# A two-layer transformer with two mixtures of experts on one core: first scores and routing moved, expert tiles in four steps of five, gathers paced, projections dense

## The chip, the cores and the metric

The kernel runs on one core of a Trainium2 chip. The metric is the device time of one execution in microseconds (us), as a median over runs. PE is TensorE, DVE is VectorE, ACT is ScalarE, POOL is GpSimd, SP is the engine that issues most transfers. All data is float32.

## The reference

The input is `x` of 8 sequences, 256 tokens each, 128 features: 2048 tokens. Layer 0 and layer 1 have the same frame: normalise, then add attention and a feed-forward network of the normalised tokens to `x`.

```python
xn = layernorm(x)
x = x + attn0(xn) + ffn0(xn)
xn = layernorm(x)
x = x + attn1(xn) + ffn1(xn)

# attn0: 16 heads of 8; q, k, v with biases; softmax(q k^T / sqrt(8)) v, then Wo and bo
# ffn0:  top 2 of 8 experts (width 176, silu(g)*u), weights are the softmax scores,
#        plus sigmoid(x w) * shared expert (width 352)
# attn1: 8 query heads of 128, one k/v head, sinusoidal positions, causal
# ffn1:  top 1 of 8 experts (width 512, gelu), times its softmax score;
#        router logits are (x wg_red^T) (wg / |wg|)^T
```

## The kernel before, in words

Tokens are 16 tiles of 128, or 4 blocks of 512. `acc` holds the residual, 16 tiles in SBUF; `xT` holds the normalised tokens transposed.

**Start.** `layernorm` takes statistics on DVE, the inverse root as a power on POOL, `xn` on DVE (L252), transposes on PE and copies into `xT` on ACT; it also writes `xn` to a DRAM table `xd` for later gathers. `l0_values` makes values `va` and router logits `lg0`. After the four blocks come the gate weights of layer 1 (`l1_gate_weights`), the router (`l0_router`: softmax, the two largest of 8), and the queries and keys of the first block (`l0_project(0)`).

**Routing.** The tokens of each expert are packed into slots of 128, at most 40 of them (`NS0`), each slot being one expert's. `routing` is a generator: counts by matmul (L312), positions by scans, then for each of two choices four rounds of one-hot tiles on DVE (L388, L395, L401) and matmuls (L406) which give `ids`, the token of each slot row. It is run between the first scores of sequence 0, two at a time, and finished before anything else begins. Then the first four slots' tokens are gathered (`slot_tokens`, indirect DMAs from POOL, L423), and weights of the first nine slots are loaded.

**Attention 0 in 64 steps.** Per sequence there are 4 head groups of 4 heads and two halves: 8 steps. A head has a strip of 32 partitions. The scores are made twice: `max_scores` (L726), one sequence ahead, whose row maxima (`max_rows`, L741) are written as a column of `mx`; `l0_augment` transposes `mx` and adds it to the queries (`qa`, L752), so that the second scores (`exp_scores`, L769) come out with the maximum taken off and transposed for the values; `exponentials` is on ACT (L781), `l0_pv` (L796) multiplies by `va`. First scores of sequence b+1 and second scores of sequence b use different strips of the array and are issued in turns. Two score buffers of two PSUM banks (`big`) serve both, three single banks (`bank`) serve all else.

**What goes between steps.** `between(step)` runs after each step's scores. Steps 3 to 43: one expert tile per step (`l0_down` of the last tile, L589; `l0_up`, L572; `l0_turn` of the next, L565). Step 43: the results of tokens 0 to 7 tiles are gathered back (`l0_back`, two gathers each), and each further one when `l0_combine` (L613) has used a buffer; there are 8 (`YT`). Steps 44 to 59: the shared expert (`shared_up` L628, `shared_down` L643). Steps 50 to 57: two `l0_combine` each. Steps 53, 55, 59: `layernorm` of layer 1. From 56: `l1_project` of its first block.

**Layer 1** follows: attention with one k/v head, the expert tiles of layer 1 in its middle, gathers, output. No line of it is in the diff but what it shares with layer 0.

Order within an engine is fixed when the program is built: a scheduler interleaves the calls within limits set by buffers and data. The order of both kernels' instructions can be listed engine by engine, and the prediction uses this.

Of the kernel before, what the change touches and what calls it, by code (L numbers as in the profile page):

```python
# [47 lines left out]

TILES = 3
SHARED = TILES + NS0 + 1  # L50
COMBINE = SHARED + 6
NORM1 = (COMBINE + 3, COMBINE + 5, COMBINE + 9)
PROJECT1 = COMBINE + 6
EPS_LN = 1e-5
# [5 lines left out]
def two_layer_kernel(  # L60
# [56 lines left out]
    minus_half = ctile([P, TPB], "minus_half")  # L117
    nc.gpsimd.memset(minus_half, -0.5)
    rev = ctile([P, NE], "rev")
    for e in range(NE):  # L120
# [43 lines left out]

    bv0_s = ctile([P, E], "bv0_s")
    bo0_s = ctile([P, E], "bo0_s")
    qb0_s = ctile([P, NG], "qb0_s")
    kb0_s = ctile([P, NG], "kb0_s")
    nc.gpsimd.dma_start(bv0_s, bv0.partition_broadcast(P))
    nc.gpsimd.dma_start(qb0_s, qb0)  # L170
# [49 lines left out]

    wqkp = wp.tile([P, 2, H0, ROW], F32, tag="wqk", name="wqkp")
    wqp, wkp = wqkp[:, 0], wqkp[:, 1]
    for padded, plain in ((wqp, wq0_s), (wkp, wk0_s)):
        nc.vector.memset(padded, 0.0)
        nc.vector.tensor_copy(padded[:, :, :D0], plain.rearrange("p (h d) -> p h d", d=D0))

# [11 lines left out]
    def layernorm(layer, blk):  # L238
# [8 lines left out]
        nc.gpsimd.tensor_scalar_add(rs, mv[:, :, 1], EPS_LN)  # L247
        nc.gpsimd.tensor_tensor(rs, rs, minus_half, ALU.pow)
        xn = work.tile([P, TPB, E], F32, tag="xn", name=f"xn_{nm}")
        ps = bank(f"lnT_{nm}")  # L250
        for t in range(TPB):
            nc.vector.tensor_scalar(  # L252
                xn[:, t, :],
                acc[:, blk * TPB + t, :],
                mv[:, t, 0:1],
                rs[:, t : t + 1],
                ALU.subtract,
                ALU.mult,
            )
            nc.tensor.transpose(ps[:, ts(t, P)], xn[:, t, :], ident)  # L260
# [188 lines left out]
    def l0_values(blk):  # L449
        for t2 in range(blk * TPB, (blk + 1) * TPB, 2):  # L450
            ps = bank(f"vg_{t2}")
            pv = ps[:, : 2 * (E + NE + 1)].rearrange("p (t c) -> p t c", t=2)
            for t in range(2):
                nc.tensor.matmul(
                    pv[:, t, :], lhsT=xT[:, ts(t2 + t, P)], rhs=wvg0_s, start=True, stop=True
                )
            for t in range(2):
                nc.vector.tensor_tensor(
                    va[:, t2 + t, :, :D0],
                    pv[:, t, :E].rearrange("p (h d) -> p h d", d=D0),  # L460
                    bv0_s.rearrange("p (h d) -> p h d", d=D0),
                    ALU.add,
                )
            nc.scalar.copy(lg0[:, ds(t2, 2), :], pv[:, :, E:])

    def l0_project(blk):
        both = work.tile([P, 2, NG, BLK], F32, tag="qk", name=f"qk0_{blk}")
        qT, kT = both[:, 0], both[:, 1]
        for g in range(NG):
            for dst, w, bias in ((qT, wqp, qb0_s), (kT, wkp, kb0_s)):  # L470
                ps = bank(f"qk0_{blk}_{g}")
                nc.tensor.matmul(  # L472
                    ps,
                    lhsT=w[:, ts(g, 4), :],
                    rhs=xT[:, ts(blk, BLK)],
                    start=True,
                    stop=True,
                )
                if w is wqp:
                    nc.vector.tensor_scalar_add(dst[:, g, :], ps, bias[:, g : g + 1])  # L480
                else:
                    nc.scalar.activation(
                        dst[:, g, :], ps, AF.Identity, bias=bias[:, g : g + 1]
                    )
        qk[blk] = (qT, kT)

    for blk in range(NBLK):
        layernorm(0, blk)
        l0_values(blk)
        nc.gpsimd.tensor_tensor(  # L490
            acc[:, ts(blk, TPB), :],
            acc[:, ts(blk, TPB), :],
            bo0_s.unsqueeze(1).to_broadcast([P, TPB, E]),
            ALU.add,
        )


    def l1_gate_weights():
# [4 lines left out]
        n1 = small.tile([NE, 1], F32, tag="wg_n1", name="wg_n1")  # L503
        nc.scalar.activation(n1, n2, AF.Sqrt)
        nc.vector.tensor_scalar_max(n1, n1, EPS_WG)
# [12 lines left out]
        nc.vector.tensor_copy(wvg1_s[:, P:], ps2[:, :NE])  # L518

    l1_gate_weights()  # L520

# [18 lines left out]
    r0 = Routing()  # L540
    routing0 = routing("l0", l0_router(), NS0, r0)

# [67 lines left out]
    def l0_combine(t):  # L610
        a = acc[:, t, :]
        for k in range(2):
            nc.vector.scalar_tensor_tensor(  # L613
                a, yt0[t][:, k, :], wr0[:, t, k : k + 1], a, ALU.mult, ALU.add
            )
        if t + YT < NTILE:
            l0_back(t + YT)

# [67 lines left out]

    def between(step):

        i = step - TILES
        if 0 <= i - 1 < NS0:  # L690
            l0_down(i - 1)
        if 0 <= i < NS0:
            l0_up(i)
        if 0 <= i + 1 < NS0:
            l0_turn(i + 1)
        if i == NS0:
            for t in range(YT):
                l0_back(t)
        blk, c = divmod(step - SHARED, len(CH) + 1)
        if 0 <= blk < NBLK:  # L700
            if c < len(CH):
                shared_up(blk, c)
            else:
                shared_down(blk)
        if 0 <= step - COMBINE < NTILE // 2:
            for t in range(2):
                l0_combine(2 * (step - COMBINE) + t)
        if step in NORM1:
            layernorm(1, NORM1.index(step))
        if step >= PROJECT1:  # L710
            for _ in range(2):
                next(project1, None)

# [22 lines left out]
    def max_rows(b, i, ps):  # L736
# [4 lines left out]
        nc.vector.tensor_reduce(  # L741
            m[:, ds(2 * half, 2), :, D0 + g], pv, AX.X, ALU.max, negate=True
        )

    def l0_augment(b):
# [3 lines left out]
        for t in range(2):  # L749
            nc.tensor.transpose(ps[:, ts(t, P)], mx[b % 2][:, t, :], ident)  # L750
        qa = work.tile([P, NG, S], F32, tag="h", name=f"qa_{b}")
        nc.vector.tensor_tensor(  # L752
            qa,
            qT[:, :, ds((b % 2) * S, S)],
            ps[:, :S].unsqueeze(1).to_broadcast([P, NG, S]),
            ALU.add,
        )
        return qa
# [71 lines left out]

    NI = 2 * NG
    l0_project(0)
    for i in range(0, NI, 2):
        pair = [big_tile(f"s1_0_{i + h}") for h in range(2)]
        issue(*(max_scores(0, i + h, pair[h]) for h in range(2)))
        for h in range(2):
            max_rows(0, i + h, pair[h])
        for _ in range(5):
            next(routing0, None)
    for _ in routing0:  # L840
        pass
    xs0[0] = slot_tokens(0, 0, r0)
    for i in range(RING0):
        l0_weights(i)
    l0_turn(0)

# [7 lines left out]
    for b in range(B):  # L854
# [4 lines left out]
        for g in range(NG):  # L859
# [3 lines left out]
            for half in range(2):  # L863
# [10 lines left out]
                eTs.append(exponentials(b, i, ps2))  # L874
                between((b * NG + g) * 2 + half)
                if half == 0 and late is not None:
                    l0_drain(*late)
                    if g == 1 and done is not None:
                        l0_finish(*done)
                        done = None  # L880
            late = (b, g, eTs, po, at)
        done = (b, at)
    l0_drain(*late)
    l0_finish(*done)


# [332 lines left out]
```

## Time and profile before

| | us |
|---|---|
| median of 3 runs | 662.15 (660.63 to 668.9) |
| the profiled execution | 647.99 |
| its span, first to last instruction | 646.1 |
| PE busy in the span | 543.4 (84%) |
| DVE busy | 400.6 (62%) |
| ACT busy | 245.1 (38%) |
| POOL busy | 140.9 (22%) |
| mean granted PE clock | 0.934 |

The profiled execution is some 14 us shorter than the median. A busy PE is not PE at its peak: where the granted clock is low, the same work is busy for longer. Shares over the span are averages over very different stages, so stages are read one by one.

### The profile page before, as it was taken

The numbers are of one execution on the slowest core, as the hardware profiler recorded it, in microseconds if no ns is written. First come the engines' busy times: TensorE is split into PE (matmuls) and PEld (weight loads), VectorE is DVE, ScalarE is ACT, GpSimd is POOL, SyncE is SP. The second block draws the span as 40 slices with busy tenths as digits, with TensorE's granted clock in tenths as the row PEclk, the third lists the DMA queues.
The fourth block names the chain that finished last, engine by engine and source line by source line (L and its number), as shares of the span: only waits on it lengthen the run. The fifth ranks groups of instructions, "written<-read, shape, count | busy, mean of one in ns | idle before, by whom it ended". The sixth has DMA issues, their size and how long they took to land.

```text
span 646.1 us, 10887 instructions
## 1 busy us (share of the span) xinstructions
PE 543.4 (84%) x3797; PEld 380.6 (59%) x3797; DVE 400.6 (62%) x959; ACT 245.1 (38%) x649; POOL 140.9 (22%) x176
## 2 busy tenths in 40 slices
PE   1779599999999999945799777989898888489786
PEld 1537547766766676513355465667577887265564
DVE  6596437766676667745875598766674423357753
ACT  1210035444544454320322433234459945133442
POOL 9200252222222200775000000004023302700000
PEclk9995589999999999988899979898899999889999
DMA  8204113432444320111000005100029993300000
GB/s 206 71 1 122 40 39 97 111 107 64 118 110 112 51 28 29 45 50 54 18 8 9 6 12 135 50 2 25 8 54 260 247 231 84 86 8 2 8 9 8
DMA packets 53414, 44.01 MB, mean 68 GB/s; under 512 B 5153, under 2 KB 48225, under 8 KB 53361
## 3 DMA queue, kind: packets, MB, share of 16 engines
q1 hardware_dynamic: 48704, 35.09, 19.8%
q0 software_dynamic: 4080, 7.97, 6.2%
q8 instruction: 30, 0.49, 0.3%
q10 hardware_dynamic: 576, 0.27, 0.2%
q14 instruction: 24, 0.19, 0.1%
HBM read 35.97 MB, written 7.34 MB: 67 GB/s over the span
## 4 chain that ended last, share of the span: by engine, by line
PE 53%; DVE 14%; issue 14%; DMA 8%; POOL 6%; ACT 5%; POOLq 0%; SPq 0%; DVEq 0%; ACTq 0%
PE s L726 6%; PE s L1022 5%; PE u L572 5%; PE o L1065 5%; PE qk L668 4%; PE qk L472 4%; PE d L589 3%; PE pv L796 3%; POOL yt L423 3%; PE pT L1058 3%; PE wo L1076 3%; ACT p L1038 3%; PE s L769 3%; PE d L965 2%; DMA yt<-yg,d_pos_l 2%
## 5 line engine op out<-in xcount | busy, mean ns | idle before, releaser
L423 POOL DMA_INDIRECT xs<-xd,d_ids_l x68 | 68.1, 1001 | 279.4 <-DVE d_ids_l L419 126.2
L781 ACT ACTIVATE eT<-s 128x1024 f32<-128x1024 f32 x64 | 65.4, 1023 | 126.3 <-PE s L769 126.3
L741 DVE TENSOR_REDUCE mx<-s 128x4 f32<-128x1024 f32 x64 | 77.9, 1218 | 18.4 <-PE s L769 12.4
L726 PE MATMUL s<-qk 32*128 32x256 f32 x512 | 78.2, 419 | 12.7 <-DVE mx L741 12.5
L1022 PE MATMUL s<-kT,qT 128*128 128x128 f32 (+1 forms) x256 | 57.7, 362 | 20.2 <-ACT p L1038 20.2
L769 PE MATMUL s<-qa,qk 32*128 32x256 f32 x512 | 71.5, 401 | 1.1 <-DVE qa L752 0.7
L726 PEld LDWEIGHTS s<-qk 32*128 32x128 f32 x512 | 46.4, 192 | 36.0 <-DVE mx L741 20.6
L423 POOL DMA_INDIRECT yt<-yg,d_pos_l x48 | 48.1, 1002 | 79.2 <-issue 46.5
L1022 PEld LDWEIGHTS s<-kT,qT 128*128 128x128 f32 x256 | 42.1, 209 | 33.5 <-ACT p L1038 27.2
L1065 PE MATMUL o<-pT,v 128*128 128x512 f32 x96 | 49.9, 630 | 9.8 <-DVE pT L1060 8.8
L1038 ACT ACTIVATE p<-s,ms 128x128 f32<-128x128 f32 (+1 forms) x128 | 52.1, 425 | 10.0 <-DVE ms L1034 8.1
L1068 ACT COPY oT<-o 128x512 f32<-128x512 f32 x32 | 18.8, 589 | 81.6 <-PE o L1065 81.6
L769 PEld LDWEIGHTS s<-qa,qk 32*128 32x128 f32 x512 | 43.2, 184 | 10.1 <-issue 6.3
L572 PE MATMUL u<-xg,gu_s 128*88 128x128 f32 x320 | 41.6, 273 | 0.0
L796 PE MATMUL pv<-eT,va 128*32 128x256 f32 x512 | 37.3, 391 | 0.6 <-ACT eT L781 0.6
L572 PEld LDWEIGHTS u<-xg,gu_s 128*88 128x88 f32 x320 | 37.0, 157 | 0.3 <-issue 0.3
L628 PE MATMUL sh<-xT,shu_s 128*128 128x512 f32 (+1 forms) x48 | 26.8, 673 | 10.5 <-DVE sg L557 10.5
L1049 DVE TENSOR_SCALAR p<-p,rec 128x128 f32<-128x128 f32 (+1 forms) x128 | 33.7, 323 | 0.7
L988 ACT ACTIVATE h<-u,own_b 128x128 f32<-128x128 f32 x96 | 26.4, 379 | 20.5 <-PE u L979 20.4
L1058 PE MATMUL pT<-ident,p 128*128 128x128 f32 x192 | 32.5, 316 | 1.6 <-DVE p L1049 1.3
L1076 PEld LDWEIGHTS wo<-wo_s,oT 128*128 128x128 f32 x256 | 30.9, 192 | 5.1 <-issue 5.1
L472 PE MATMUL qk<-xT,wqkp 128*128 128x512 f32 x64 | 33.6, 679 | 0.0
(208 smaller groups left out, 916.6 us busy)
## 6 DMA issues: line engine op xcount, KB each, us to landing
w_up<-in_w_dram SPq DMA_DIRECT2D x30, 256.0 KB
gu_s<-in_gu_dram SPq DMA_DIRECT2D x40, 176.0 KB
w_down<-in_w_dram SPq DMA_DIRECT2D x18, 256.0 KB
yg<-ys SPq DMA_DIRECT2D x16, 256.0 KB
dn_s<-in_dn_dram SPq DMA_DIRECT2D x40, 88.0 KB
xd<-xn SPq DMA_DIRECT2D x8, 256.0 KB
bias<-in_b_dram SPq DMA_DIRECT2D x24, 64.0 KB
xs<-xd,d_ids_l POOLq DMA_INDIRECT x68, 3.0
```

The source lines that it names most:

```text
L423: nc.gpsimd.indirect_dma_start(out=dst, out_offset=None, in_=table, in_offset=bass.IndirectOffsetOnAxis(ap=index, axis=0), bounds_check=ta ...
L472: nc.tensor.matmul(ps, lhsT=w[:, ts(g, 4), :], rhs=xT[:, ts(blk, BLK)], start=True, stop=True,)
L572: nc.tensor.matmul(ps[:IC, ts(c, P)], lhsT=gu0_s[:, i % RING0, c, :], rhs=xg0.get(i), start=True, stop=True,)
L726: nc.tensor.matmul(pv[:, jj, t, :], lhsT=qT[r : r + ROW, g, ds(o + t * P, P)], rhs=kT[r : r + ROW, g, ds(o, S)], start=True, stop=True,)
L741: nc.vector.tensor_reduce(m[:, ds(2 * half, 2), :, D0 + g], pv, AX.X, ALU.max, negate=True)
L769: nc.tensor.matmul(pv[:, jj, c, :], lhsT=kT[r : r + ROW, g, ds(o + c * P, P)], rhs=qa[r : r + ROW, g, :], start=True, stop=True,)
L781: nc.scalar.activation(eT.rearrange("p j c q -> p (j c q)"), ps, AF.Exp, scale=SC0)
L796: nc.tensor.matmul(po[ds(ROW * j, ROW), ts(g % 2, S)], lhsT=va_flat[:, ds(o, ROW)], rhs=eTs[j // 2][:, j % 2, c, :], start=(c == 0), stop= ...
L1022: nc.tensor.matmul(sc[:, hh, :], lhsT=qT[:, 4 * hg + hh, ds(o + t * P, P)], rhs=kT[:, ds(o, nk)], start=True, stop=True,)
L1038: nc.scalar.activation(p[:, hh, :], sc[:, hh, :], AF.Exp, bias=ms[:, hh : hh + 1], scale=SC1, accum_out=sums[:, hh : hh + 1],)
L1058: nc.tensor.transpose(ps[:, ts(hh, P)], p[:, hh, ts(c, P)], ident)
L1065: nc.tensor.matmul(po, lhsT=v1[:, 2 * b + c, :], rhs=pT[:, c, :], start=(c == 0), stop=(c == t))
```

## The change

- **First scores**: the maxima pass of sequence 0 is issued inside the loop over the four normalisations, two of its eight pieces per block, right after `l0_values` of the block; `l0_project(0)` follows the first normalisation.
- **Routing between steps**: `routing` is advanced once per place, a place being half a step (128 in all), over places 0 to 15; at 16 it is finished, the first gathers and the weight loads are issued.
- **Tiles 5 in 4 steps**: tile i stands at place 20 + 8i/5 (rounded down), so five tiles in eight places; the last `l0_down` is at place 84.
- **Paced gathers**: `l0_back(t)` at place 88 + 3t/2, `l0_combine(t)` eight places later, for each t.
- Shared expert one piece per two places from 86; normalisations of layer 1 at 102, 108, 114; first projections of layer 1 one per place from 106. `l1_gate_weights` moves to place 30, except what the scheduler pulls forward; its root becomes a power on POOL instead of a square root on ACT.
- **Dense projections with masked copies**: queries and keys of a block come from one matmul each instead of four each; four copies per result multiply with a 0/1 column (`own`) and add a bias. `l0_augment` becomes four operations with a mask column (`turn`), one per head group.
- **Norms on ACT**: `xn` is made by ACT as scale times input plus offset; DVE makes the offset.
- `va` is copied by ACT without bias (the value bias is multiplied by `Wo` once and added to `bo0_s`), `lg0` by DVE.

```diff
+    wq0_p, wk0_p = (wqkp[:, n].rearrange("p j g d -> p (j g d)") for n in range(2))
...
+        off = small.tile([P, TPB], F32, tag="ln_off", name=f"off_{nm}")
+        nc.vector.scalar_tensor_tensor(off, mv[:, :, 0], -1.0, rs, ALU.mult, ALU.mult)
...
-            nc.vector.tensor_scalar(
+            nc.scalar.activation(
                 xn[:, t, :],
                 acc[:, blk * TPB + t, :],
-                mv[:, t, 0:1],
-                rs[:, t : t + 1],
-                ALU.subtract,
-                ALU.mult,
+                AF.Identity,
+                bias=off[:, t : t + 1],
+                scale=rs[:, t : t + 1],
             )
...
+                nc.scalar.copy(
+                    va[:, t2 + t, :, :D0], pv[:, t, :E].rearrange("p (h d) -> p h d", d=D0)
                 )
-            nc.scalar.copy(lg0[:, ds(t2, 2), :], pv[:, :, E:])
+            nc.vector.tensor_copy(lg0[:, ds(t2, 2), :], pv[:, :, E:])
...
+        for n, (dst, w) in enumerate(((qT, wq0_p), (kT, wk0_p))):
+            ps = bank(f"qk0_{blk}_{n}")
+            nc.tensor.matmul(ps, lhsT=w, rhs=xT[:, ts(blk, BLK)], start=True, stop=True)
+            for g in range(NG):
+                if n == 0:
+                    nc.vector.tensor_scalar(
+                        dst[:, g, :], ps, own[:, g : g + 1], qkb[:, n, g : g + 1], ALU.mult, ALU.add
                     )
...
-        nc.scalar.activation(n1, n2, AF.Sqrt)
+        nc.gpsimd.tensor_tensor(n1, n2, half_power, ALU.pow)
...
+    for n in range(TILES - 4):
+        at_place(n, lambda: next(routing0, None))
+    at_place(TILES - 4, lambda: [None for _ in routing0] and None)
+    at_place(TILES - 4, l0_begin)
+    at_place(TILES - 1, l0_turn, 0)
+    for i in range(NS0 + 1):
+        at_place(TILES + i * 8 // 5, l0_tile, i)
...
+    for t in range(NTILE):
+        at_place(BACK + t * 3 // 2, l0_back, t)
+        at_place(COMBINE + t * 3 // 2, l0_combine, t)
...
+        for g in range(NG):
+            nc.vector.scalar_tensor_tensor(
+                qa[:, g, :],
+                ps[:, :S],
+                turn[:, g : g + 1],
+                qT[:, g, ds((b % 2) * S, S)],
+                ALU.mult,
+                ALU.add,
+            )
...
+    for blk in range(NBLK):
+        layernorm(0, blk)
+        if blk == 0:
+            l0_project(0)
+        l0_values(blk)
+        first_scores(2 * blk)
...
+    routing0 = routing("l0", l0_router(), NS0, r0)
```

## The prediction

> **What bounds the kernel now.** I read the table of busy time by stage first, cutting the span where the work changes (first second scores at 89.3 us, first expert tile 97.1, last tile 255.1, end of attention 0 at 362), then the timelines at the two places where PE is not full, then the groups for prices.
>
> ```profile
> core 0: us, PE busy (x) PEld busy (x) DVE busy (x) ACT busy (x) POOL busy (x), PEclk, DMA share, GB/s
> 0.00:40.00 40.00, 23.43 (x84) 15.62 (x84) 24.49 (x99) 9.39 (x21) 19.48 (x52) 1.00 0.44 112
> 40.00:79.70 39.70, 28.13 (x127) 22.61 (x128) 25.88 (x71) 0.13 (x1) 2.88 (x3) 0.59 0.23 65
> 79.70:89.30 9.60, 9.60 (x18) 3.84 (x16) 4.21 (x5) 2.19 (x4) 5.73 (x7) 0.73 0.17 43
> 89.30:97.10 7.80, 7.31 (x74) 4.44 (x73) 2.47 (x3) 3.91 (x5) 3.54 (x4) 1.00 0.13 34
> 97.10:255.10 158.00, 153.08 (x1542) 107.57 (x1538) 107.85 (x173) 73.70 (x166) 31.85 (x32) 1.00 0.33 83
> 255.10:362.00 106.90, 85.76 (x633) 45.49 (x629) 66.50 (x155) 29.76 (x37) 36.05 (x38) 0.94 0.11 31
> 362.00:646.00 284.00, 236.14 (x1332) 181.04 (x1332) 169.19 (x455) 126.01 (x416) 41.41 (x42) 0.94 0.27 70
> ```
>
> Three stages matter. Up to 89.3 us nothing of attention's 64 steps has begun, ACT is nearly unused from 40 on, and PE runs at a granted clock of 0.59. The tile stage is PE's: 153.08 of 158.00 us. The tail has 21 us in which PE does nothing. Layer 1 (284.0 us) is not touched. The timelines show what the first and third wait for:
>
> ```profile
> 76.21 1.19 POOL L423 DMA_INDIRECT xs<-xd,d_ids_l  x1 [52.14 <-DVE d_ids_l L419]
> ...
> 79.57 0.27 ACT L567 COPY xg<-xg 128x128 f32<-128x128 f32 x1 [39.99 <-PE xg L565]
> ...
> 290.79 0.26 POOL L247 TENSOR_SCALAR rs<-mv 128x4 f32<-128x4 f32 x1
> ...
> 293.46 2.02 PE L628 MATMUL sh<-xT,shu_s 128*96 128x512 f32 x2 [10.49 <-DVE sg L557]
> ...
> 318.57 0.48 PE L726 MATMUL s<-qk 32*128 32x256 f32 x2 [3.43 <-DVE mx L741]
> ```
>
> The first two lines: everything waits for the chain of routing, DVE and PE by turns, to end at 76 us. The last three: 24 gathers, 1.3 us apart on POOL from 259.74, delay the inverse root `rs` until 290.8; DVE stands in `l0_combine` and then before L252 meanwhile, and PE stops for 10.49 us. I add PE's idle over the tail's waits on DVE: 1.50 + 10.49 + 1.96 + 1.92 + 3.43 = 19.3 us. Prices come from the groups:
>
> ```profile
> L741 DVE TENSOR_REDUCE mx<-s 128x4 f32<-128x1024 f32 x64 | 77.9, 1218 | 18.4 <-PE s L769 12.4 <-PE s L726 5.8
> L472 PE MATMUL qk<-xT,wqkp 128*128 128x512 f32 x64 | 33.6, 679 | 0.0
> L480 DVE TENSOR_SCALAR qk<-qk,qb_s 128x512 f32<-128x512 f32 x16 | 12.0, 751 | 14.7 <-PE qk L472 14.3
> L482 ACT ACTIVATE qk<-qk,kb_s 128x512 f32<-128x512 f32 x16 | 11.0, 687 | 25.8 <-PE qk L472 25.8
> ```
>
> **What the Trainium skill says.** "TensorE: Matmul & The Clock Gate", Part 1: PE's clock is gated to half after an idle window of about 3.4 us and opens after a busy one as long. The trace agrees: 0.59 in the routing stage, 1.00 in the tile stage, and back at full after some 5 us of dense projections from 79.75. The same page, on the array's architecture: ACT and DVE are strict queues; so an instruction that waits holds all behind it, as the 10.49 us show. "PSUM — Partial Sum Buffer", bank collisions: ACT and DVE may not use one bank at once, so reads of one bank are put in order; the trace has ACT's `lg` copies waiting 10.5 us in total for DVE's `va`, of the same bank. "ScalarE: Activation LUTs", what a table load costs: 186 ns + 0.833 ns per element, 93 ns more for each pointer operand, neighbours overlapping by 93 ns. For L482, one pointer, that gives 706 ns (687 measured).
>
> **The change part by part.**
>
> *Start, until the second scores begin: 89.3 to 43.* Three small DMAs more stand ahead on POOL's queue (0.55 us each), so `wg_s` lands 1.7 us later than its 10.95; the new power for the gate weights stands ahead of the first `rs` on POOL and waits for it. First `rs` at some 14.5 (11.8 before), `xn` on ACT by 16.3: with two pointers an estimate from the ScalarE page is 479 ns, 386 apart, against 408 on DVE. Transposes and `xT`: 17.4. One dense matmul, cold: two records were 1.7 us at half clock; so q at 19.1 and k at 20.8. Four k copies on ACT (estimate 799 ns, 706 apart) to 23.8; the `va` copies stand behind them, DVE's `lg` behind those, the first row maximum behind `lg`: 25. Eight maxima are 9.8 us of DVE, but a pair's buffers come free only as it goes: 2.4 for two maxima plus about 1.7 for the scores that PE can only then finish, 4.1 a pair; the last ends at 39.6. Transposing `mx`, the block-1 projection and the first `qa` piece ahead of the scores: 3.4. Sum 43, bounds 39 and 48.
>
> *Ten steps with routing: 46 us.* These are steps 0 to 9. In the listed order, DVE has there 10 maxima (12.2), 8 pieces of `qa` (nearest row 128x256 at 0.42: 3.4), 4 q copies (3.0), two and a half normalised outputs (2.9), and of router and routing 8 one-hot rows at 0.685 (5.5), 16 columns at 0.32 (5.1), some 30 operations of 128x128 at 0.2 apart (6) and small ones (5): 43.1 us. PE's work is less at full clock: 1.8 a step (below) plus 8 rounds of L406 at 1, plus projection 1.7: 28 us. At half clock it is 55. I take DVE's sum plus 0.3 us a step for its waits on PE's L406: 46. Bounds 40 and 56.
>
> *Tile stage, 32 steps instead of 41: 158.0 to 142.* Between 111.96 and 176.80, 16 steps with 16 tiles and one projection (7.3) took 64.84: 3.6 a step. From the timeline, scores of both kinds are 1.15 a step, `pv` 0.5, the rest 0.15: 1.8; so a tile is 1.8 too. With 1.25 tiles: 4.05. I add 0.3: a tile's down waits 1.57 us after its up for ACT and DVE, and where two tiles have only one group of scores (1.1) or `pv` (1.0) between them, PE now waits. 32 x 4.35 = 139.2; the remaining two projections cost 2 matmuls at 0.85 each instead of 8 (7.3): 3.4. DVE per step is 1.22 + 1.25 x 0.84 + about 0.8 = 3.1 and ACT 2.3, both under 4.35. Weights: 264 KB per 3.5 us is 75 GB/s, below the 100 reached before. Bounds 134 (no added wait) and 152 (0.6 a step). Starting at 89, it ends at 231 instead of 255.1, so 22 steps remain.
>
> *Tail: 106.9 to 89.* Gathers start at step 44, after the last results, and a tile's pair (2.6 us) comes every three quarters of a step (3 us); each combine is four steps behind its gathers, some 16 us, against 2.6 us to land. POOL's `rs` then stands behind a gather or two. So the 19.3 us of stalls go, and 3.7 us of matmuls that ran slow after them (L628 2.02 for 1.12, L643 3.36 for 2.94, and the like). 85.76 - 3.7 = 82; one step and a half more of plain attention 2.7; 4.5 for waits that remain: DVE has 66.5 us here, so it is late next, and `xn` on ACT holds exponentials while it waits for `rs`. Bounds 85 and 98.
>
> *Edits at nothing.* `off` (four small DVE operations per layer) and the square root's table load (1.28 at 5.66, before any use of ACT): hidden by loads; uncovered, 1 us. Moving `l1_gate_weights` takes two small matmuls into a tile step. `qa` in pieces costs 0.5 us more DVE a sequence, in the cover of first scores; uncovered, 4 us over all. In layer 1 PE's listed order is the same for the last 241 rows; 284.
>
> **Sum.** 43 + 46 + 142 + 89 + 284 = 604 of span, 42 less than 646.1; the profiled execution would go from 647.99 to about 606. The three runs' median is 14.2 above the profiled execution; I take the difference over: 662.15 - 42 = 620, rounded to 619.
>
> **Rivals.**
>
> *Routing takes the gain back.* The ten steps run at half clock, 5.6 us each, and tiles wait 0.6 a step: 48 + 56 + 152 + 92 + 284 = 632 of span, some 14 gained: 647. For it: 0.59 granted in today's routing stage. Against: there PE had nothing else to do; now scores of two kinds and `pv` lie between.
>
> *All stages reach PE's work or DVE's sum.* 40 + 41 + 135 + 86 + 284 = 586: 602. For it: today's tile stage is 97% PE. Against: it adds a quarter to what every queue holds per step.
>
> *Slower: the clock stays at half into the tile stage.* One mechanism: waits between denser tiles keep the gate from opening. Each us of tile work at full clock then costs one more; PE has 130 us of it, and the 42 gained are gone once 42 us of it ran so, about 84 us of time. If all did, 604 + 130 = 734: 749. For it: 40 us at 0.59 now. Against: 5 us of dense work opened the gate at 85, and tiles are dense.
>
> That the gathers are not paced after all (they wait for buffers of combines that DVE reaches late) leaves some 12 of the 19.3 us: 631; inside the range.
>
> **How the numbers follow.** Forecast 0.58, routing rival 0.17, full-speed rival 0.20, slower 0.05. The range, 598 to 641, takes in the full-speed rival and most of the routing one; its ends are about those of the bounds added with half their weight. A change is told from none at about 2%, 13 us: faster 0.92 (all of the forecast and full-speed cases, most of the routing rival), same 0.04, slower 0.04.
>
> **What would show each step.** First second scores near 43 us and the last maximum of sequence 0 near 40; first expert tile (up) near 89; the granted clock from 43 to 89 above 0.7; tile stage about 142 with PE above 93%; no PE wait over 3 us in the tail; layer 1 still 284. It is wrong if the first tile is later than 100, or if the tail again has a wait near 10 us.

## The result: 1.5% faster, not 6.5%, and the tail and the chip are why

| | before | after |
|---|---|---|
| median of 20 runs each | 669.31 us (660.63 to 681.44) | 657.11 us (652.18 to 666.77) |
| ratio after to before, 95% interval | | 0.9845 (0.9814 to 0.9876) |
| the profiled execution, its span | 647.99, 646.1 (shown in the prediction) | 657.19, 655.4 |

Forecast were 619 us and a range of 598 to 641. Ratios compare fast runs with fast runs, while medians take in every run, so that a ratio can differ a little from the quotient of two medians.

The executions fall into two kinds, told apart by what the kernel before takes on the same chip: 660 to 685 us (called kind A here) or 640 to 650 us (kind B, but for one run of 731.24). The experiments saw three chips of kind A and two of kind B, each in one sitting; the text says "kind of chip", though a passing state of the machine is not excluded. The 20 runs above are of kind A; the profile of before that the prediction was worked out from agrees with kind B. Within one experiment all kernels ran on one chip, so that a ratio is safe; where two experiments on different chips are compared, the text says so. The two profiles of the table are not of the same kind. Both kernels were therefore profiled again on the other kind.

The stages of the kernel after, first on A (the kernel as timed above), then on B. Each line gives the stretch, its length, then busy time of PE, of its weight loads, of DVE, ACT and POOL, the granted clock, and DMA. The cuts are: second scores begin, first expert tile, last expert tile, end of attention 0. So the third line is the tile stage, the fourth the tail, the fifth layer 1.

```profile
core 0: us, PE busy (x) PEld busy (x) DVE busy (x) ACT busy (x) POOL busy (x), PEclk, DMA share, GB/s
0.00:45.80 45.80, 28.04 (x146) 17.36 (x146) 28.02 (x91) 16.50 (x43) 21.93 (x57) 0.97 0.38 97
45.80:88.60 42.80, 36.98 (x309) 23.90 (x308) 35.66 (x95) 13.07 (x15) 4.14 (x4) 0.84 0.22 63
88.60:248.20 159.60, 138.44 (x1322) 99.00 (x1321) 95.25 (x171) 66.86 (x159) 35.96 (x37) 0.96 0.33 84
248.20:364.80 116.60, 97.90 (x663) 52.74 (x662) 66.85 (x154) 34.98 (x50) 36.16 (x38) 0.87 0.10 28
364.80:655.40 290.60, 241.36 (x1336) 184.06 (x1332) 167.50 (x452) 128.03 (x420) 41.48 (x42) 0.93 0.26 69
```

```profile
0.00:45.90 45.90, 28.08 (x146) 17.72 (x146) 28.07 (x91) 16.49 (x43) 21.86 (x57) 0.96 0.37 96
45.90:91.10 45.20, 39.40 (x308) 25.24 (x307) 35.97 (x95) 13.17 (x15) 3.66 (x4) 0.77 0.20 58
91.10:230.50 139.40, 132.30 (x1325) 95.56 (x1321) 94.67 (x171) 66.67 (x159) 36.42 (x37) 1.00 0.37 96
230.50:343.90 113.40, 94.62 (x661) 50.73 (x661) 66.80 (x154) 34.92 (x50) 36.10 (x38) 0.88 0.10 29
343.90:624.60 280.70, 234.29 (x1337) 179.31 (x1332) 168.06 (x452) 127.86 (x420) 41.35 (x42) 0.95 0.26 71
```

And the kernel before on A. On B, cut at the same events, it takes 97.2 us up to the first tile, then 158.3, 106.1 and 284.4.

```profile
0.00:84.80 84.80, 59.31 (x227) 40.96 (x227) 54.42 (x174) 11.72 (x25) 27.76 (x60) 0.76 0.32 88
84.80:92.80 8.00, 7.32 (x74) 4.43 (x73) 2.46 (x3) 3.92 (x5) 3.99 (x4) 1.00 0.11 33
92.80:258.50 165.70, 158.05 (x1544) 109.41 (x1541) 107.77 (x174) 73.92 (x167) 31.85 (x32) 1.00 0.30 79
258.50:376.60 118.10, 96.59 (x625) 51.31 (x625) 66.31 (x155) 29.59 (x37) 36.20 (x38) 0.87 0.10 28
376.60:665.90 289.30, 239.41 (x1336) 183.07 (x1332) 168.41 (x455) 126.17 (x416) 41.42 (x42) 0.94 0.25 69
```

What to see: the first two stages came as forecast on either kind (45.8 and 45.9 us for 43; 42.8 and 45.2 for 46). The tile stage is 139.4 on B, with PE 95% busy, for a forecast of 142; on A it is 159.6, and PE does nothing for 21 us of it, against 7 on B. The tail is 113.4 and 116.6 for a forecast of 89: that term failed everywhere. On B the change gains 6.1 us up to the first tile and 18.9 in the tile stage; the tail, which now holds more of attention, takes 7.3 back; layer 1, which is not touched, is 3.7 shorter.

**The tail, on B.** POOL, DVE and ACT around the first norm of layer 1, from the timelines:

```profile
264.51 0.99 POOL L466 DMA_INDIRECT yt<-yg,d_pos_l  x1 [0.30 <-issue]
265.53 0.26 POOL L289 TENSOR_SCALAR rs<-mv 128x4 f32<-128x4 f32 x1
...
266.95 0.16 DVE L292 SCALAR_TENSOR_TENSOR off<-mv,rs 128x4 f32<-128x4 f32 x1 [11.28 <-POOL rs L290]
...
267.15 1.65 ACT L296 ACTIVATE xn<-acc,off,rs 128x128 f32<-128x128 f32 x4 [10.38 <-DVE off L292]
```

The gather at 264.51 is the last of 24 in a row, 1.3 us apart, from 234.60. The root `rs` stands behind them; DVE waits 11.28 us for it, ACT 10.38, and PE stops for want of both. It is the stall of the kernel before over again, where PE stopped for 10.49 us. The waits of PE in this stretch, total, times, longest:

```profile
PE sh L654 <- DVE sg L585: 9.3, 2, 7.1
PE s L768 <- DVE mx L783: 5.5, 3, 3.4
```

The order of POOL's instructions is fixed when the program is built, and this trace shows it: the gathers of tiles 0 to 11, two each, stand ahead of the first root, and nothing ties a gather to its place in the program. This could have been read before any run.

**The stall on A.** From the timeline of the kernel after, near the first expert tile, on A:

```profile
88.06 0.60 PE L814 MATMUL s<-qa,qk 32*128 32x256 f32 x4
...
91.45 1.23 DVE L783 TENSOR_REDUCE mx<-s 128x4 f32<-128x1024 f32 x1 [4.66 <-PE wo L870]
...
92.90 1.00 POOL L466 DMA_INDIRECT xs<-xd,d_ids_l  x1 [0.31 <-issue]
95.08 1.02 ACT L826 ACTIVATE eT<-s 128x1024 f32<-128x1024 f32 x1 [7.45 <-remote]
```

The same maxima and exponentials on B:

```profile
91.22 1.23 DVE L783 TENSOR_REDUCE mx<-s 128x4 f32<-128x1024 f32 x1 [1.44 <-PE s L814]
91.33 1.02 ACT L826 ACTIVATE eT<-s 128x1024 f32<-128x1024 f32 x1 [1.48 <-PE s L814]
```

On A the scores are done at 88.7 by PE's records; DVE begins the maxima at 91.45 and ACT the exponentials at 95.08, just after POOL's eighth gather in a row ended at 93.90. On B both begin within 0.2 us of the scores' end. The profile names PE's L870 for the wait of DVE; on B the same maxima start before that matmul does (93.25), so they do not need it. "remote" is a release that no record explains. No profile of kind B has one.

### The profile page after: what moved, and what is told of

The parts are those of the page before. It is cut to its first block, busy times and chain, and to the rows that moved or that the text cites. A ratio compares the mean times of both kernels' runs of the same rounds, so it can differ in the third digit from the quotient of the medians.

```text
span 655.4 us, 10882 instructions
## 1 busy us (share of the span) xinstructions
PE 542.7 (83%) x3766; PEld 377.1 (58%) x3766; DVE 393.3 (60%) x961; ACT 259.4 (40%) x686; POOL 139.7 (21%) x177
## 4 chain that ended last, share of the span: by engine, by line
PE 60%; DVE 12%; ACT 11%; issue 7%; POOL 5%; another core or an unknown queue 4%; DMA 1%; SPq 0%; POOLq 0%; ACTq 0%; DVEq 0%
PE s L768 8%; PE o L1125 5%; PE s L1082 5%; PE u L600 5%; PE pv L841 5%; PE wo L1136 4%; PE qk L694 4%; PE s L814 4%; PE d L617 4%; ACT p L1098 3%; PE pT L1118 3%; DVE mx L783 3%; PE qk L512 2%; PE u L1039 2%
## 5 line engine op out<-in xcount | busy, mean ns | idle before, releaser
L466 POOL DMA_INDIRECT xs<-xd,d_ids_l x64 | 64.3, 1004 | 271.5 <-DVE d_ids_l L462 123.8
L768 PE MATMUL s<-qk 32*128 32x256 f32 x512 | 85.8, 437 | 23.8 <-DVE mx L783 19.1
L814 PE MATMUL s<-qa,qk 32*128 32x256 f32 x512 | 79.4, 429 | 1.1 <-DVE qa L795 0.7
L1125 PE MATMUL o<-pT,v 128*128 128x512 f32 x96 | 52.8, 662 | 10.9 <-ACT oT L1128 7.2
L1098 ACT ACTIVATE p<-s,ms 128x128 f32<-128x128 f32 (+1 forms) x128 | 52.2, 426 | 13.4 <-DVE ms L1094 10.4
L814 PEld LDWEIGHTS s<-qa,qk 32*128 32x128 f32 x512 | 47.1, 199 | 12.3 <-issue 5.6
L1128 ACT COPY oT<-o 128x512 f32<-128x512 f32 x32 | 18.9, 589 | 81.6 <-PE o L1125 71.2
L841 PE MATMUL pv<-eT,va 128*32 128x256 f32 x512 | 43.4, 409 | 1.2 <-ACT eT L826 1.2
L585 DVE SCALAR_TENSOR_TENSOR sg<-sg,u 88x256 f32<-88x256 f32 x40 | 16.6, 416 | 43.2 <-ACT sg L584 33.2
L617 PE MATMUL d<-dn_s,h 88*128 88x128 f32 x160 | 29.3, 306 | 12.4 <-issue 8.1
L617 PEld LDWEIGHTS d<-dn_s,h 88*128 88x128 f32 x160 | 22.1, 199 | 26.2 <-issue 20.1
L1090 DVE TENSOR_TENSOR s<-s,mask 128x512 f32<-128x512 f32 x32 | 22.2, 694 | 19.7 <-PE s L1082 10.4
```

The lines of the kernel that those rows point to most:

```text
L466: nc.gpsimd.indirect_dma_start(out=dst, out_offset=None, in_=table, in_offset=bass.IndirectOffsetOnAxis(ap=index, axis=0), bounds_check=ta ...
L617: nc.tensor.matmul(ps[:, :P], lhsT=h0[i][:, c, :], rhs=dn0_s[:, i % RING0, c, :], start=(c == 0), stop=(c == 1),)
L768: nc.tensor.matmul(pv[:, jj, t, :], lhsT=qT[r : r + ROW, g, ds(o + t * P, P)], rhs=kT[r : r + ROW, g, ds(o, S)], start=True, stop=True,)
L814: nc.tensor.matmul(pv[:, jj, c, :], lhsT=kT[r : r + ROW, g, ds(o + c * P, P)], rhs=qa[r : r + ROW, g, :], start=True, stop=True,)
L841: nc.tensor.matmul(po[ds(ROW * j, ROW), ts(g % 2, S)], lhsT=va_flat[:, ds(o, ROW)], rhs=eTs[j // 2][:, j % 2, c, :], start=(c == 0), stop= ...
L1098: nc.scalar.activation(p[:, hh, :], sc[:, hh, :], AF.Exp, bias=ms[:, hh : hh + 1], scale=SC1, accum_out=sums[:, hh : hh + 1],)
```

## The experiments

Each text below was put down before its run. A theory or a rival named afterwards is one of that text.

**Again, both kernels (A).** No edit.

> The kernel before, unchanged, for a second profiled execution. The first one (span 646.1 us) was shorter than every one of its 20 timed runs (660.63 to 681.44). Theory 1: it was an unrepresentative execution, and a second one has a span of 658 to 672, with waits of several us that its records do not explain (named 'remote' or 'issue') as the kernel after has. Theory 2: the kernel before has none of these, and its span is again 643 to 650.

> The kernel after, unchanged, for a second profiled execution (the first: span 655.4, unexplained waits of 4 to 9 us at 87.6, 256, 269, 553, 558 and 565 us). Theory 1: the waits belong to the execution; a second one has them at other places, or fewer, and its span is 648 to 662. Theory 2: the change causes them; they stand at the same instructions (steps 10 and 44 to 46), within 2 us in size.

Spans 665.9 and 657.0. The first profile of before was indeed no measure for these 20 runs. The waits of the kernel after stood at the same instructions again (89.8, 256.7, 270.8, 557 us), as theory 2 of the second text says, so they are not chance. But the change is not their only cause: the kernel before had such waits too, in layer 1 at 569 to 581 us, against theory 2 of the first text. Set side by side on A, the change gave 4.2 us up to the first tile, 6.1 in the tile stage, 1.5 in the tail, and layer 1 lost 1.3.

**Normalised output back on DVE (A).** `xn` as before, no `off`.

> The kernel after with one part undone: the normalised output is made on DVE again, as subtract and multiply, and the offset goes. Theory 1: in the tail ACT stands before the output, waiting for the inverse root, with exponentials behind it (waits of 4.60 and 8.98 us); on DVE the maxima stand behind it instead, and DVE gets 16 x 0.41 us more, so the time is 2 to 6 us longer. Rival: DVE is waiting there for the root anyway, exponentials come free, and the time is 3 to 6 us shorter.

666.1 us, ratio 0.9958 (0.993 to 0.9986), against 0.9845 with it on ACT: 1.1% or 7.6 us longer, the direction of theory 1 and more than its 6. Tail and layer 1 grew (116.6 and 290.6 with ACT); in layer 1, where the edit has little to do, the 2.9 us are not explained:

```profile
248.30:369.30 121.00, 99.30 (x661) 52.45 (x662) 69.69 (x163) 30.47 (x38) 36.92 (x38) 0.86 0.09 27
369.30:662.80 293.50, 243.07 (x1336) 185.50 (x1332) 169.03 (x455) 126.05 (x416) 41.52 (x42) 0.92 0.25 68
```

**Gathers truly paced (A, then B).** POOL first copies one element of the step's exponentials into the buffer, so that the gather can't be issued sooner.

```diff
         yt0[t] = work.tile([P, 2, E], F32, tag="yt", name=f"yt0_{t}", bufs=YT)
+        for k in range(2):
+            nc.gpsimd.tensor_copy(yt0[t][:, k, 0:1], now["eT"][:, 0, 0, 0:1])
```

> The kernel after with the gathers of layer 0's results really tied to their places: POOL first copies one element of the step's exponentials into each buffer that the gather then overwrites, so that a gather can't be issued before its step; this also puts 2 to 8 gathers fewer ahead of each inverse root of layer 1. Theory 1: the root standing behind bursts of 8 gathers costs the tail some 8 us; with the pacing these waits of DVE and ACT go, 6 to 10 us shorter. Rival: the tail is long because of unexplained waits and a low clock, and the pacing moves the time by under 2 us.

641.3 us, ratio 0.9604 (0.955 to 0.9659): 16 us less than the kernel after by the ratios, more than theory 1 gave. Its waits near 256 and 270 us were gone (1.3 us of DVE were left at 263), so two causes were mixed in one edit: the order of the root, and the run of gathers. In its profiled execution, the fastest of six, the tail is 101.6 us, 15 shorter; layer 1, which the edit does not touch, is 8 shorter too.

**All long runs broken up (A, then B).** The second group of token gathers waits for two tiles; the 16 of layer 1's results are tied to six attention steps, in the order in which they are used.

> The kernel with the gathers of layer 0's results tied to their steps, and now all other long runs of gathers broken up too: the second group of four token gathers waits for two expert tiles, and the 16 gathers of layer 1's results are tied to six attention steps, at most four at once. Theory 1, a long run of gathers on POOL is itself what holds DVE and ACT back (they are released late from PE's finished scores only while POOL issues more than four or five gathers in a row: at 88 to 95, 256 to 276 and 553 to 570 us in the kernel after): the stall near 88 to 97 us goes (5 to 9 us with the slow clock behind it) and layer 1 loses 5 to 14 us; 8 to 18 us less than the paced kernel's 641.3. Rival: the late releases are due to PE or to the data they wait for, not to POOL; within 3 us of 641.3, with the stall at 88 to 97 us still there.

631.18 us, ratio 0.9354 (0.9274 to 0.9434): 2.5% below the paced kernel's, in theory 1's span. But this is another chip than the paced kernel's, so the 2.5% are not the edit's alone; the two medians differ by 10.1 us. The stall at the first tile went, as theory 1 says, and yet the last tile ends at 247.0 where the paced kernel's ended at 247.5. Its tile stage is

```profile
92.40:247.00 154.60, 137.22 (x1322) 97.72 (x1321) 95.45 (x171) 66.68 (x159) 36.43 (x40) 0.98 0.33 87
```

with PE idle for 17.4 us of it, where the same kernel on B takes 139.3. So most of what A costs in the tile stage does not come from the first eight gathers.

**The kernel before, its gathers paced (A).** The copy into the buffer as above, the old calls taken out, and:

```diff
+        for t in range(NTILE):
+            if step == SHARED - 1 + t * 7 // 8:
+                l0_back(t)
```

> The kernel before with one thing changed: the gathers of layer 0's results are tied to the steps 43 to 56, one tile's pair a step, instead of eight tiles at once and then two a combine. Theory 1: the run of 24 gathers costs the tail of the kernel before as much as it costs the kernel after: 12 to 20 us less than 669. Rival: in the kernel before the run delays only the inverse root, some 10 us of PE idle, and something else is late next: 3 to 8 us less.

663.71 us, ratio 0.9839 (0.9771 to 0.9906), 11 us: between the two. Against the kernel before on another chip of kind A, the tail fell from 118.1 to 106.1, and PE's idle time in it from 21.5 to 13.4:

```profile
264.20:370.30 106.10, 92.73 (x627) 49.07 (x625) 66.67 (x155) 29.40 (x37) 41.38 (x70) 0.90 0.11 31
```

On A, pacing alone gives the kernel before as much as the whole change gave. The pacing was not complete: POOL came to the first gathers late, and ten of them ran from 268.45 to 281.78 us with only the small copies between. At their end, at 283.17, ACT had stood for 5.89 us with no release in the records.

**Needless work on POOL (A).** 52 memsets in a row, and 8 gathers in a row, in the tile stage.

> The kernel after with two pieces of work on POOL that nobody needs, in the tile stage where POOL is idle: 52 memsets (some 10 us in a row) after step 22, and 8 gathers of tokens in a row (10.4 us) after step 33, each held back until that step's exponentials exist. Theory 1, gathers in a row hold DVE and ACT back: nothing happens beside the memsets; beside the 8 gathers DVE and ACT have waits of 3 us or more that the records of PE don't explain, PE stops, and its clock drops. Rival a, POOL busy in any way does it (a shared port): the same beside the memsets. Rival b, POOL has no part: nothing at either place, PE over 85% busy in both.

Windows of this run: the memsets, then the end of the gathers, then what followed.

```profile
161.00:175.00 14.00, 13.37 (x137) 10.22 (x138) 10.34 (x20) 6.46 (x16) 10.79 (x53) 1.00 0.39 112
...
222.00:228.00 6.00, 0.09 (x1) 0.00 (x0) 0.20 (x1) 0.00 (x0) 4.47 (x6) 0.74 0.22 44
228.00:240.00 12.00, 9.02 (x59) 6.83 (x59) 4.25 (x7) 3.70 (x9) 1.90 (x2) 0.56 0.37 46
```

Beside the memsets (13.6 us in a row) PE is 95% busy. Beside the gathers (8, and 4 of the next group behind them) PE, DVE and ACT all do nothing for 6 us, and then PE's clock is near half. Rivals a and b fall.

**A tile's down projection later (A).** `l0_down(i - 2)` for `l0_down(i - 1)`.

> The kernel after with each expert tile's down projection one tile later (two tiles after its up projection instead of one). Theory 1: in the tile stage PE waits for the hidden activations of the tile just before (its weight queue stands 27.6 us, 52 times, before the down projection between 105 and 248 us); that goes, the tile stage takes 148 instead of 160, and the time is 7 to 14 us shorter. Rival: the wait moves to the next thing in the queue (the maxima that free the score buffers, or weights); within 3 us of the kernel after.

662.99 us, ratio 0.9735 (0.9605 to 0.9866): by time inconclusive, as the interval overlaps that of the kernel after. The waits of PE between 110 and 245 us, of the kernel after and then of this one:

```profile
PE d L617 <- issue: 7.9, 17, 1.7
PE s L768 <- DVE mx L783: 4.1, 4, 1.4
```

```profile
PE s L768 <- DVE mx L783: 5.9, 7, 1.4
...
PE d L617 <- issue: 0.5, 1, 0.5
```

The wait for the hidden activations went, that for the maxima grew, and PE's busy time in these 135 us stayed (119.84 and 120.83): the rival. On B, the kernel after has the order as it was and 3.7 us of that wait in all.

**Root ahead of the later gathers, and dense projections undone (B).** The first: buffers of tiles 8 to 15 get an element of the root before their gathers, which also stand three steps later in the program; the 16 gathers ahead stay a run. The second: four matmuls each for queries and keys, zero columns in the weights.

```diff
+        if t >= YT:
+            for k in range(2):
+                nc.gpsimd.tensor_copy(yt0[t][:, k, 0:1], roots[1, (t - YT) // TPB][:, 0:1])
```

> The kernel after with only POOL's order changed: the inverse root of the first norm of layer 1 stands ahead of the gathers of tiles 8 to 11, that of the second ahead of tiles 12 to 15 (one element of each buffer is first copied from the root); the run of 16 gathers at 252 us stays. It splits the 16 us that pacing brought. Theory 1: most of them came from breaking the run of gathers, and only the waits behind the root (some 7 us of PE idle at 288 to 292 and 310 to 318 us) are due to the order: 3 to 7 us shorter than the kernel after. Rival: the order of the root behind the gathers was the whole cost: 13 to 16 us shorter.

> The kernel after with the dense projections undone: four matmuls each for queries and keys of a block, with zero columns in the weights, as before; masks and places stay. Theory 1: PE has 6 more matmuls of 0.85 us per block, and the tile stage and the first scores are bound by PE: 12 to 20 us longer than the kernel after. Rival: PE is idle 15 us of the tile stage anyway and copies set the pace of a projection: under 6 us longer.

These fell on B, where the kernel before took 645.64 us: ratios 0.9571 (0.9519 to 0.9622) and 0.9808 (0.9761 to 0.9856). The first has no kernel after beside it and is repeated below. The second set against the kernel after's 0.971 on the other chip of kind B is 1.0% or some 6 us longer, just beyond the rival and half of theory 1. Its start and its tile stage:

```profile
0.00:48.60 48.60, 29.86 (x158) 18.79 (x158) 28.24 (x94) 16.81 (x43) 21.91 (x57) 1.00 0.34 91
...
91.60:238.90 147.30, 141.45 (x1349) 99.79 (x1345) 95.69 (x171) 67.35 (x159) 35.84 (x36) 1.00 0.35 91
```

The tile stage has 9.2 us more of PE, and is 7.9 longer: two blocks with 6 matmuls more each, at 0.85 (10.2). Theory 1 counted a third block that lies before this stage, where DVE sets the time.

**A second probe (B, then A).** 6 gathers in a row; 8 plain 64 KB loads issued from POOL; 6 gathers in pairs with 8 copies between.

> The kernel after with three more pieces of needless work on POOL in the tile stage: 6 gathers in a row after step 16, 8 plain 64 KB loads issued from POOL after step 23, and 6 gathers after step 29 in pairs with 8 small copies (2 us or more) between the pairs. Theory 1, the rate and number of gathers in a row decide: a stop of PE (over 2 us) only beside the six in a row and where they join the next group's four; none beside the pairs. Rival a, every transfer issued from POOL does it: the same beside the plain loads. Rival b, only the number outstanding counts, not the gaps: the pairs stop PE too.

> The kernel after with 6 gathers in a row after step 16, 8 plain loads issued from POOL after step 23, and 6 gathers in pairs with copies between after step 29, none of them needed, once more: its first run fell where the kernel before takes 641 to 650 us, and nothing stopped anywhere. Where before takes 660 or more, theory 1 (only runs of gathers hold DVE and ACT back): PE stops for over 2 us beside the six that the next group's four join, and not beside the plain loads or the pairs. Rival a: beside the plain loads too. Rival b: beside the pairs too. Where before takes 640 to 650 it only repeats: PE over 90% busy at all three.

> The kernel before, unchanged, on the same chip as the run beside it, for its stages. Where before takes 640 to 650 us: the tail of attention 0 at 104 to 108 and the tile stage at 157 to 160 us, as in the profile before. Where it takes 660 or more: 116 to 120 and 164 to 168.

On B the six with the next four behind them, and the plain loads:

```profile
122.00:137.00 15.00, 14.14 (x151) 11.07 (x150) 10.06 (x19) 8.04 (x21) 10.76 (x16) 1.00 0.57 154
...
149.00:156.00 7.00, 7.00 (x76) 5.21 (x76) 5.89 (x11) 3.23 (x8) 5.80 (x17) 1.00 0.55 156
```

On A the same two:

```profile
133.00:149.00 16.00, 12.64 (x118) 9.14 (x117) 7.04 (x15) 5.50 (x15) 10.81 (x16) 0.89 0.42 113
...
166.00:172.00 6.00, 6.00 (x63) 4.36 (x66) 4.89 (x11) 2.92 (x8) 5.34 (x16) 1.00 0.56 157
```

On B ten gathers in a row stop nothing. On A PE stands for 3.4 of 16 us there, one stop of 2.1 us among it, and no stop lies beside the plain loads: theory 1 on A, by a small margin, since PE is idle for 2.3 of the 13 us just before as well. Rival a falls for loads as short as these: the eight took 4.4 us in all, the ten gathers 14, and a longer run of plain loads was not tried. Beside the pairs no stop reaches 2 us, but PE is 84% busy (12.61 of 15), so pairs are not free on A. The kernel before on this chip: tile stage 166.5, tail 119.7, as expected of A.

**On one chip of kind B, with the kernel after beside them.**

> The kernel after, unchanged, beside the kernel before on the same chip once more. In the last three runs the kernel before took 641 to 650 us, as its first profile, and no trace of them has an unexplained wait; in the earlier ones it took 660 to 685 and all traces have them. Theory 1, the waits beside gathers belong to the chip a run falls on: where before takes about 645, the kernel after has none, its tile stage takes 138 to 142 us, and it takes 620 to 628, a ratio of 0.96 to 0.975; where before takes 665 or more, the ratio is 0.98 to 0.99 with the waits at the same places as ever. Rival: the ratio is 0.985 on every chip.

> POOL's order changed so that the inverse roots stand ahead of the later gathers, on the same chip as the kernel after. Its ratio of 0.957 has no kernel after from the same chip beside it. Theory 1: the order is worth 3 to 7 us against the kernel after on either kind of chip. Rival: its whole gain was the chip; within 2 us of the kernel after.

> The gathers of layer 0's results tied to their steps, on the same chip as the kernel after. Theory 1: on a chip with the unexplained waits 13 to 18 us shorter than the kernel after, on a chip without them only what the order of the roots brings, 3 to 8 us. Rival: 13 to 18 us on either.

> All long runs of gathers broken up, on the same chip as the kernel after. Theory 1: on a chip with the unexplained waits 4 to 12 us shorter than with layer 0's results alone paced; on a chip without them the two are within 4 us of each other. Rival: 4 to 12 us shorter on either.

| on B, before 644.06 us | us | ratio (95%) | tail | layer 1 |
|---|---|---|---|---|
| after | 625.86 | 0.971 (0.9659 to 0.9762) | 113.4 | 280.7 |
| root ahead of later gathers | 617.86 | 0.9598 (0.9538 to 0.9659) | 104.2 | 279.7 |
| paced | 612.96 | 0.9522 (0.9458 to 0.9586) | 99.4 | 281.0 |
| all runs broken up | 605.56 | 0.9426 (0.9388 to 0.9465) | 97.7 | 275.9 |

The change is worth 2.9% on B and 1.5% on A, as theory 1 of the first text had it. More than half of what pacing brings on B is the order of the root: 8.0 of 12.9 us, where theory 1 of the second text had 3 to 7. The 12.9 lie just below the 13 to 18 of the third text's rival, and above the 3 to 8 of its theory 1. A run of gathers thus costs on B too, mainly by what stands behind it; which wait the remaining 4.9 us are was not tried apart. Breaking up layer 1's gathers was to bring nothing more on B, and brought 7.4 us, 5.1 of them in layer 1. The trace of the paced kernel shows a wait there of about that size:

```profile
PE o L1129 <- DVE pT L1124: 8.1, 1, 8.1
```

```profile
523.49 1.00 POOL L466 DMA_INDIRECT yt<-yg,d_pos_l  x1 [0.30 <-issue]
526.08 0.62 DVE L1188 SCALAR_TENSOR_TENSOR acc<-yt,score,acc 128x128 f32<-128x128 f32 x2 [7.45 <-DMA yt<-yg,d_pos_l]
```

The gather at 523.49 is the thirteenth of a row of 16, that of tile 12; a gather lands 2.6 us after its issue here (the median), so by the times it is the one that DVE stands 7.45 us for, with copies for PE behind it. The program asks for tiles 12 and 13 first. In DVE's order as built seven other tiles were combined before, and then it was the turn of tile 12. The broken-up version gathers in the order of use; its longest wait of DVE for such a transfer is 2.7 us, and PE's wait of 8.1 us is gone from its trace. What the new order and what the breaking up did was not separated. It is the version that beats both kernels: 0.9354 on A, 0.9426 on B.

## Why the prediction was right or wrong, step by step

- **Start, 43:** 45.8 and 45.9, inside its bounds of 39 to 48. **Ten steps, 46:** 42.8 and 45.2; the clock was 0.84 and 0.77, above the 0.7 named. Both lengths held, and the first tile came near the forecast 89 (88.6 and 91.1). That is only 4 to 6 us sooner than before: the gain is that ten steps of attention lie behind it. The 46 is in part luck: it was 43.1 us of DVE and 3 of its waits, and on B DVE was busy for 36.0 and idle for 9.2, while PE was busy for 39.4.
- **Tile stage, 142:** right on B in its parts too: PE is busy 132.3 us where 133 were summed, and idle 7.1 where 9.6 were, so the 0.3 us of wait per step was if anything too much. On A 159.6; there the term lacks waits that the profile used, being of kind B, doesn't contain: 7.45 us of ACT at the first eight gathers, and at five of the eight later groups of four some 2 us of DVE with no release in the records, 10.0 in all. The broken-up version without the first of these still takes 154.6, so the groups of four, or something not found, carry most of it. The kernel before pays less for it there (165.7 against 158.3 on B).
- **Tail, 89:** the step that failed. "Gathers start at step 44 ... and a tile's pair ... comes every three quarters of a step" read a place in the program as a time. POOL has nothing to wait for at a place, so it issues as fast as buffers come free; "`rs` then stands behind a gather or two" should have been 24. Of the 19.3 us of PE's stalls on DVE, 17.4 stayed on B (9.3, 5.5 and 2.6 of small ones). Of the 24.4 us that the tail is above its forecast there, 14.3 are PE idle (18.8 for 4.5) and 9.9 PE busy (94.6 for 84.7), at a clock of 0.88. The text named this case at its end, left 12 us of the stalls, too few, and gave it no chance of its own. With the gathers really paced the tail is 99.4, 10 above the forecast still: PE is busy 89.6 where 82 plus 2.7 were summed, at a clock of 0.95, and idle 9.8 where 4.5 were.
- **Layer 1, 284:** 280.7 on B, 290.6 on A.
- **The sum and its anchor.** On B the span is 624.6 for a forecast of 604; 24.4 of it is the tail, the other terms are together 4 below. Then "the three runs' median is 14.2 above the profiled execution; I take the difference over" treated a difference between two kinds of chip as a constant. From B to A the kernel after loses 20.2 us in the tile stage, 3.2 in the tail and 9.9 in layer 1, and gains 2.5 ahead of the tiles; the kernel before loses 7.4, 12.0 and 4.9, and gains 4.4. The spans differ by 30.8 and by 19.8, so the constant carried over was too small for both, and by far for the kernel after. With it the forecast of the span on A is 618; the 37 us up to the measured 655.4 are 24.4 of tail, 16.6 of a constant too small, less the 4.
- **Edits at nothing:** the norms on ACT were counted as a risk in the tail; they are worth 1.1% on A. The slower rival (half clock into the tile stage) did not happen on B at all; in the profile on A half clock came in the tile stage only from 94 to 104 us, behind the first stop, and from 128 to 131.

**What stays open.** What makes a chip of kind A hold DVE and ACT back beside gathers, and whether it is the chip or a state of it. PE's ends are modelled in the profile, so whether its results or only their release came late cannot be told. The probes exclude POOL being busy as such and a short run of plain transfers issued by POOL. The number of packets is no likely cause: the profile counts 32 for a gather and 32 for a plain load of 64 KB (256 more in the first probe for its 8 gathers, 640 more in the second for 12 gathers and 8 loads). Whether it is the scattered rows, the making of the gathers on POOL or the length of the run was not separated. All times here are of executions that the profiler recorded; whether recording has a part was not tried.

## What to carry to other kernels

A place in a program is not a time: an engine with nothing to wait for runs ahead to its next full buffer, so read in its listed order what stands behind a burst, and pace it with a real dependency (one copied element is enough, if the engine does not come to the burst late, as in the kernel before). Before a sum of stages is set against a median, make sure that profile and median come from the same chip, for instance by the profiled execution against the range of the times; here 647.99 lay 12.6 below the lowest of them. And try gathering in the order in which the results are used.

## What the runs showed of the hardware that was not expected

On chips of kind A, gathers in a row on POOL delay DVE and ACT with PE's work already recorded as done: DVE by some 2 us beside four in a row, ACT by 7.45 us beside eight, and by 15.2 us (until 286.56 in the second repeat of the kernel before) beside 16. The size is not set by the number alone: ten in a row stopped PE for 2.1 us at most in the second probe. On kind B up to 24 in a row delay nobody who doesn't wait for POOL; none of its eight profiles has a wait that is put down to "remote".

After such a stop PE also runs at half clock. In the first probe:

```profile
222.00:224.00 2.00, 0.09 (x1) 0.00 (x0) 0.00 (x0) 0.00 (x0) 1.39 (x3) 1.00 0.12 35
224.00:226.00 2.00, 0.00 (x0) 0.00 (x0) 0.00 (x0) 0.00 (x0) 1.69 (x2) 0.72 0.22 66
...
232.00:234.00 2.00, 0.53 (x2) 0.56 (x3) 1.46 (x3) 1.46 (x3) 0.00 (x0) 0.50 0.23 49
...
238.00:240.00 2.00, 2.00 (x21) 1.46 (x13) 1.23 (x1) 1.18 (x2) 0.00 (x0) 0.86 0.00 0
```

PE's last work ends near 222.1, and by an estimate from the clock of these slices it halves at 224.9 and is full again at 238.6. PE worked and waited by turns from 228 on and was busy without a break only from about 233.5. The Trainium skill's "TensorE: Matmul & The Clock Gate", Part 1, puts the gate at an idle window of about 3.4 us and as long a busy one; the trace agrees in kind, with 2.8 us of idle time before the drop and some 5 us of unbroken work before the recovery.
